# Layer 3 of a graph network: the edges' factors in pieces of 8 tiles, the one-hot ahead of a wait, and gathers 8 quads ahead of PE

## The chip, the cores and the metric

The kernel runs on one core of a Trainium2 chip. The metric is the time of one execution in device microseconds, taken as the median of several runs. The core's engines are TensorE (PE, matmuls; PEld is its weight load), VectorE (DVE), ScalarE (ACT), GpSimd (POOL) and SyncE (SP). Each engine works through its own instructions in order; between engines they wait for one another with semaphores.

## The reference, cut to what matters

Four layers pass messages along 262144 edges between 8192 nodes of 32 features; each ends in a residual sum and a layer norm. The edges are sorted by their target. The change concerns the fourth (layer 3):

```python
def _L3_gnn_ref(node_attr, edge_index, edge_sh, edge_feat, W1, b1, W2, b2, si_w0, si_w1):
    h = jax.nn.relu(edge_feat @ W1 + b1)
    w = (h @ W2 + b2).reshape(e, 4, MUL, MUL)                  # MUL = 8
    w_000, w_011, w_101, w_110 = (w[:, 0], w[:, 1], w[:, 2], w[:, 3])
    s = node_attr[:, :MUL]
    v = node_attr[:, MUL:].reshape(n, MUL, 3)
    s_e, v_e = s[src], v[src]
    sh0, sh1 = edge_sh[:, 0], edge_sh[:, 1:4]
    m0 = ALPHA * (jnp.einsum('ei,eio->eo', s_e * sh0[:, None], w_000)
                  + C110 * jnp.einsum('eim,em,eio->eo', v_e, sh1, w_110))
    m1 = ALPHA * (jnp.einsum('ei,em,eio->eom', s_e, sh1, w_011)
                  + jnp.einsum('eim,eio->eom', v_e * sh0[:, None, None], w_101))
    out0 = jax.ops.segment_sum(m0, dst, num_segments=n) + SI_SCALE * (s @ si_w0)
    out1 = ...
x = _layernorm(x + _L3_gnn_ref(x, edge_index, edge_attr_4, edge_attr_32, ...), axis=-1)
```

So each edge gathers the row of its source (s, 8 numbers, and v, 8 x 3), has 256 weights of its own from a small network over its 32 features, and sends 32 numbers to its target. The products of the row with the edge's four numbers `sh` (s x sh0, the sum of v x sh1, v x sh0) don't need the weights: these are the "factors".

## The kernel before

The edges lie in tiles of 128 (one edge on each partition). Layer 3 has 2048 tiles, in 512 quads of 4 tiles (`q`), in 64 batches of 32 tiles or 8 quads (`s`).

**GpSimd (POOL)** fetches the source rows with one indirect DMA for each tile (L383, in `indirect`), four for each quad. `fetch_rows(q)` issues those of quad q after a wait for PE's weight matmuls of quad q - AHEAD, with AHEAD = 12: so the gathers of the first 12 quads need no wait for PE. `gathers` also waits, at the first tile of each group of 8, until the buffer of the group is free (`taken`; there are four buffers of 32 tiles) and until the group two before has landed.

**PE** has three kinds of matmuls for layer 3. At even q it computes the hidden layer of quads q + 2 and q + 3 (`hidden`, L883), which ACT turns into the activations (relu, L891). For each q it makes the weights of the quad (L907, 4 matmuls of 256 columns, into one of two `w` banks); they wait for ACT and until VectorE has freed the bank (`w_free`). Then it adds up the messages of quad q - 4 (L916, one-hot matrices times products), after VectorE's mark of quad q - 2 at the latest.

**VectorE (DVE)** does in round q, in this order: at q % 8 == 6 the factors of the next batch (below); the last product of quad q - 2 (L931); the reduce of quad q - 1 (L936); then it waits for PE's weights of quad q, multiplies them with the factors (L944, L947, three times L951), and builds the one-hot matrices of the quad (`one_hot`, L505). The mark behind the one-hot is what frees the `w` bank, lets the aggregation go on, and, at the end of a group, frees the gather buffer. Every second round it also takes two quads' sums out of PSUM (L973, L974, L976).

**The factors** of a batch (`factors`, L825 to L836) are six instructions over all 32 tiles: the scale of `sh`, three products, a reduce and a scale. They wait until all four groups of gathers of the batch have landed. One set is computed in each 8 quads, so 64 in all.

**Windows.** Every 64 quads, in the same round as a set of factors (q % 8 == 6), PE shifts the sums to their targets (`windows`, L495) and VectorE and ACT normalize a stripe of nodes (`normalize`, from L454).

**SP** loads the edges' features and `sh` three batches ahead (`fetch`).

**Before the first quad** a loop of 16 rounds (L852 to L858, the "z loop") goes from PE to ACT to PE to VectorE and adds each node's own part. The first hidden layer (L883) comes after it, while POOL's first gathers are under way.

Of the kernel before, what the change touches and what calls it, by code (L numbers as in the profile page):

```python
# [16 lines left out]
OP = mybir.AluOpType  # L17
# [4 lines left out]
P = 128  # L22
# [6 lines left out]
ALPHA = 0.25  # L29
C110 = 1.0 / np.sqrt(3.0)  # L30
# [7 lines left out]
WT = 32  # L38
# [107 lines left out]
def raw_layers(tc, x, a, w0, w1, b1, w2, si, m, bad):  # L146
    nc = tc.nc
    PE, V, A, G, S = (Flow(tc, e, n) for e, n in ((nc.tensor, "pe"), (nc.vector, "dve"), (nc.scalar, "act"),
                                                  (nc.gpsimd, "pool"), (nc.sync, "sp")))
    bank, arena = m["bank"], m["arena"]  # L150
    x_a, x_b, src, row, rel = (m[k] for k in ("x_a", "x_b", "src", "row", "rel"))
    ident, shift, stack, small = (m[k] for k in ("ident", "shift", "stack", "small"))
    iota_s = m["iota_s"]
    ytab, xtab, hist, amat, cmat = (m[k] for k in ("ytab", "xtab", "hist", "amat", "cmat"))
# [37 lines left out]
    cut = Carve()  # L192
# [8 lines left out]
    xg = cut(4, WT, D)  # L201
    oh = cut(4, GT, P, dt=BF)
# [5 lines left out]
    cut = Carve(8192)  # L208
# [5 lines left out]
    cut = Carve()  # L214
# [211 lines left out]
    def gathers(table, ix, s, t0=0, n=WT):  # L426

        if t0 == 0:
            state["n"] += 1
        k = (state["n"] - 1) % 4  # L430
        for t in range(t0, t0 + n):
            ld = g_ld[k][t // TP]
            if t % TP == 0:
                G.after(taken[k][t // TP])
                if len(under_way) >= LAG:
                    G.after(under_way[-LAG])
            indirect(xg[:, k, t, :], table[:, :], ix[:, s * WT + t:s * WT + t + 1]).then_inc(ld.sem, 16)
            ld.n += 16
            if t % TP == TP - 1:
                under_way.append(ld.mark())  # L440
        return k, under_way[-(WT // TP):]
# [62 lines left out]
    def one_hot(o, t, n):  # L504
        return V.e.tensor_tensor(o, iota[:, None, :].to_broadcast([P, n, P]),  # L505
                                 rel[:, t:t + n, None].to_broadcast([P, n, P]), op=OP.is_equal)
# [254 lines left out]
    ef = cut(3, 2, 512)  # L761
    sh = cut(3, WT, 4)
    a0 = cut(2, WT, 16)
    vs = cut(WT, 8, 3)
    a1 = cut(WT, 8)
    vm = cut(2, WT, 3, 8)
    MW = 344
    NP, NO = 6, 6
# [36 lines left out]
                                         a["ea4"][:, 4 * s * WT:4 * (s + 1) * WT]))  # L805
        batch[s] = dict(e=e_in, s=s_in)

    AHEAD = 12
    rows = {}

    def fetch_rows(q):

        if q < NQ:
            G.after(quad.get(q - AHEAD, {}).get("w"))
            rows[q // 8] = gathers(xtab, src, q // 8, q % 8 * 4, 4)

    def factors(s):

        k, landed = rows[s]
        b = batch[s]  # L820
        b["xg"] = k
        shv = sh[:, s % 3]
        u = s % 2
        V.after(b["s"])
        sm = V.mark(V.e.tensor_scalar(shv, shv, ALPHA, None, op0=OP.mult))  # L825
        V.after(*landed, sm)
        xv = xg[:, k]
        v = xv[:, :, 8:].rearrange("p t (i m) -> p t i m", m=3)
        vmk = V.mark(V.e.tensor_tensor(vs, v, shv[:, :, None, 1:4].to_broadcast([P, WT, 8, 3]), op=OP.mult))
        V.e.tensor_tensor(a0[:, u, :, 0:8], xv[:, :, 0:8], shv[:, :, 0:1].to_broadcast([P, WT, 8]), op=OP.mult)  # L830
        V.e.tensor_tensor(vm[:, u].rearrange("p t m i -> p t i m"), v,
                          shv[:, :, None, 0:1].to_broadcast([P, WT, 8, 3]), op=OP.mult)
        V.after(vmk)
        rm = V.mark(V.e.tensor_reduce(a1, vs, AX.X, OP.add))
        V.after(rm)
        b["f"] = V.mark(V.e.tensor_scalar(a0[:, u, :, 8:16], a1, float(C110), None, op0=OP.mult))  # L836


    V.after(c_in)
# [59 lines left out]
    for q in range(NQ + LAG3 + 2):  # L899
# [18 lines left out]
            quad[c]["a"] = PE.mark(ins)  # L918

        prev = (V.sem, V.n)  # L920
        if q % 8 == 6 and q // 8 + 1 < NS:
            s = q // 8 + 1
            factors(s)
        V.after(prev)
        if q < NQ:
            V.after(batch[q // 8]["f"])
        V.after(quad.get(q - NP, {}).get("a"))
        ins = None
        if 0 <= q - 2 < NQ:
# [8 lines left out]
        if q < NQ:  # L938
            k, wp = quad[q]["k"]
            s, u = q // 8, (q // 8) % 2  # L940
            qs = slice((q % 8) * 4, (q % 8) * 4 + 4)
            pq = p[:, q % NP]
            V.after(quad[q]["w"])
            V.e.tensor_tensor(pr[:, q % 2].rearrange("p t (o i) -> p t o i", i=8),  # L944
                              wp[:, :, 128:192].rearrange("p t (o i) -> p t o i", i=8),
                              xg[:, batch[s]["xg"], qs, None, 0:8].to_broadcast([P, 4, 8, 8]), op=OP.mult)
            V.e.tensor_tensor(pq[:, :, 0:128].rearrange("p t (o k) -> p t o k", k=16),  # L947
                              wp[:, :, 0:128].rearrange("p t (o k) -> p t o k", k=16),
                              a0[:, u, qs, None, :].to_broadcast([P, 4, 8, 16]), op=OP.mult)
            for mm in range(3):  # L950
                V.e.tensor_tensor(pq[:, :, 128 + 64 * mm:192 + 64 * mm].rearrange("p t (o i) -> p t o i", i=8),  # L951
                                  wp[:, :, 192:256].rearrange("p t (o i) -> p t o i", i=8),
                                  vm[:, u, qs, mm, None, :].to_broadcast([P, 4, 8, 8]), op=OP.mult)
            ins = one_hot(oh[:, q % NO], 4 * q, 4)
        if ins is not None:
            d = V.mark(ins)
            if q < NQ + 2:
# [498 lines left out]
```

## Time and profile before

| | us |
|---|---|
| median of 3 runs | 7668.28 (7660.74 to 7670.0) |
| the profiled execution | 7583.78 |
| its span in the profile | 7581.8 |
| DVE busy in the span | 4352.7 (57%) |
| PE busy in the span | 5254.6 (69%) |
| POOL busy in the span | 3996.6 (53%) |

The profile is that of one execution, which was some 1.1% faster than the median. Layer 3's first gather starts at 4522.57, and the layer ends with the span.

A line of the timeline has the start in us, the time it took, the engine, the line of the kernel, the operation, what it writes and reads, how many it stands for, and in brackets the idle time before it and who ended that. A line of the groups has busy time and the mean in ns after the first bar, and the idle time before the group's instructions after the second. "issue" is time in which the profile shows no wait; "remote" is a releaser that the profile can't place.

### The profile page before, as it was taken

Reading aid. Unit: us, or ns where it says so; the run is one execution under the profiler, and the core shown is the slowest. Engines: PE = TensorE matmul, PEld = TensorE weight load, DVE = VectorE, ACT = ScalarE, POOL = GpSimd, SP = SyncE. Lnnn points to the kernel's source line nnn. Section 1 sums busy time; section 2 is a strip of 40 time slices with the busy share of each in tenths; the row PEclk is TensorE's granted clock in tenths of the full one; section 3 lists DMA queues with packets and bytes.
Section 4 is the critical chain, followed back from the end, with each engine's and each line's share of the span. In section 5 each row is a group of like instructions: output and inputs, shape, how many; then the busy total and the mean of one; then the engine's idle time right before and its main releaser. Section 6 shows DMA issues by size and latency. Waiting matters only on the chain.

```text
span 7581.8 us, 85791 instructions
## 1 busy us (share of the span) xinstructions
PE 5254.6 (69%) x34036; PEld 3717.5 (49%) x34036; DVE 4352.7 (57%) x8312; ACT 1629.6 (21%) x2812; POOL 3996.6 (53%) x4174
## 2 busy tenths in 40 slices
PE   5326665556555665654544867889989988888998
PEld 2115555555555555553222434555555555555555
DVE  3336676677676767764000005666666667666676
ACT  3213333333333333332000001111111111111111
POOL 3466565656566666650000016666666666666663
PEclk7557677777777777777777877999998999899989
DMA  8416655556555555668999971111111111111111
GB/s 285 149 36 145 144 150 139 145 144 152 145 145 145 144 151 138 152 142 279 428 431 428 386 289 18 28 23 25 24 24 24 24 24 24 24 24 24 25 24 20
DMA packets 290731, 999.29 MB, mean 132 GB/s; under 512 B 99021, under 2 KB 175886, under 8 KB 250638
## 3 DMA queue, kind: packets, MB, share of 16 engines
q1 hardware_dynamic: 155742, 916.89, 32.2%
q0 software_dynamic: 134144, 73.67, 12.2%
q8 instruction: 269, 4.41, 0.2%
q10 hardware_dynamic: 432, 3.15, 0.1%
q14 instruction: 144, 1.18, 0.1%
HBM read 521.39 MB, written 471.99 MB: 131 GB/s over the span
## 4 chain that ended last, share of the span: by engine, by line
PE 55%; another core or an unknown queue 11%; DMA 11%; issue 9%; DVE 8%; ACT 5%; POOL 0%; SPq 0%; DVEq 0%; ACTq 0%; POOLq 0%
PE bank L571 18%; PE bank L916 14%; PE bank L907 11%; DMA f_arena<-famat 7%; PE bank L657 3%; PE bank L883 3%; DMA f_arena<-fcmat 3%; ACT f_arena L576 3%; PE bank L730 2%; PE bank L733 2%; ACT f_arena L575 2%; DVE f_arena L951 1%; DVE f_arena L505 1%; PE bank L495 1%
## 5 line engine op out<-in xcount | busy, mean ns | idle before, releaser
L383 POOL DMA_INDIRECT f_arena<-fxtab,f_src x2048 | 1967.3, 961 | 2099.2 <-DVE f_arena L787 1089.0
L383 POOL DMA_INDIRECT f_arena<-fytab,f_row x2048 | 1962.0, 958 | 1280.5 <-issue 548.2
L571 PE MATMUL bank<-f_arena 64*128 64x128 f32 x16384 | 1566.7, 365 | 963.4 <-ACT f_arena L576 682.8
L571 PEld LDWEIGHTS bank<-f_arena 64*128 64x128 f32 x16384 | 1463.3, 272 | 1100.6 <-issue 938.7
L916 PE MATMUL bank<-f_arena 128*128 128x344 f32 x4096 | 1420.3, 489 | 65.4 <-issue 63.7
L907 PE MATMUL bank<-f_arena 65*128 65x256 f32 x4096 | 1075.3, 405 | 176.2 <-issue 161.0
L916 PEld LDWEIGHTS bank<-f_arena 128*128 128x128 f32 x4096 | 842.8, 207 | 509.3 <-issue 217.5
L907 PEld LDWEIGHTS bank<-f_arena 65*128 65x128 f32 x4096 | 785.2, 198 | 559.3 <-issue 361.0
L575 ACT ACTIVATE f_arena<-bank 128x512 bf16<-128x512 f32 x1024 | 613.0, 599 | 1925.4 <-PE bank L571 816.8
L891 ACT ACTIVATE f_arena<-bank,f_arena 64x512 f32<-64x512 f32 x512 | 351.3, 686 | 2500.1 <-remote 1001.6
L557 DVE TENSOR_TENSOR f_arena<-bank,f_arena 128x1024 f32<-128x1024 f32 x256 | 313.3, 1224 | 759.8 <-PE bank L657 440.4
L505 DVE TENSOR_TENSOR f_arena<-bank,f_rel 128x512 f32<-128x512 f32 (+1 forms) x768 | 660.9, 861 | 139.9 <-ACT f_arena L537 127.7
L944 DVE TENSOR_TENSOR f_arena<-bank,f_arena 128x256 f32<-128x256 f32 x512 | 214.7, 419 | 845.0 <-PE bank L907 324.4
L576 ACT ACTIVATE f_arena<-bank 128x512 f32<-128x512 f32 x1024 | 611.7, 597 | 0.0
L559 DVE TENSOR_TENSOR f_arena<-bank,f_arena 128x2048 f32<-128x2048 f32 x256 | 586.6, 2291 | 8.8
L951 DVE TENSOR_TENSOR f_arena<-bank,f_arena 128x256 f32<-128x256 f32 x1536 | 552.0, 416 | 0.0
L730 PE MATMUL bank<-f_arena,f_x_b 128*32 128x256 f32 x4096 | 293.2, 457 | 344.9 <-DMA f_arena<-famat 344.9
L657 PE MATMUL bank<-f_arena 128*128 128x96 bf16 x2048 | 216.7, 222 | 357.7 <-issue 215.5
L730 PEld LDWEIGHTS bank<-f_arena,f_x_b 128*32 128x32 f32 x4096 | 145.1, 131 | 481.8 <-DMA f_arena<-famat 318.0
L454 DVE TENSOR_TENSOR f_lnf<-bank,f_x_b 128x256 f32<-128x256 f32 x8 | 3.4, 425 | 615.0 <-PE bank L710 615.0
L947 DVE TENSOR_TENSOR f_arena<-bank,f_arena 128x512 f32<-128x512 f32 x512 | 348.8, 681 | 0.0
L657 PEld LDWEIGHTS bank<-f_arena 128*128 128x128 bf16 x2048 | 122.0, 104 | 404.5 <-issue 260.2
(133 smaller groups left out, 3532.6 us busy)
## 6 DMA issues: line engine op xcount, KB each, us to landing
famat<-f_arena SPq DMA_DIRECT2D x256, 1024.0 KB
fcmat<-f_arena SPq DMA_DIRECT2D x256, 512.0 KB
fytab<-f_arena SPq DMA_DIRECT2D x64, 1024.0 KB
f_arena<-fytab,f_row POOLq DMA_INDIRECT x2048
f_arena<-fxtab,f_src POOLq DMA_INDIRECT x2048
f_arena<-laid_ea SPq DMA_DIRECT2D x64, 512.0 KB
f_arena<-laid_ea SPq DMA_DIRECT2D x64, 64.0 KB
f_arena<-laid_xT ACTq DMA_DIRECT2D x1, 1024.0 KB, 8.9
```

The lines of the kernel that those rows point to most:

```text
L383: return G.e.indirect_dma_start(out=dest, out_offset=None, in_=table, in_offset=bass.IndirectOffsetOnAxis(ap=ix, axis=0))
L505: return V.e.tensor_tensor(o, iota[:, None, :].to_broadcast([P, n, P]), rel[:, t:t + n, None].to_broadcast([P, n, P]), op=OP.is_equal)
L559: V.e.tensor_tensor(oh_l[:, b], iota[:, None, :].to_broadcast([P, 16, P]), meta_l[:, pp, k0:k0 + 16, None].to_broadcast([P, 16, P]), op=OP ...
L571: ins = PE.e.matmul(bank[:, bk + h, :].rearrange("p (c s j) -> p c s j", s=64, j=4)[:, :, :, j], oh_l[hs_, b, 4 * q + j, :], oh_k[hs_, b, ...
L575: A.e.activation(st_c[:, b, q], bank[:, bk:bk + 2, 0:256], AF.Copy)
L576: bank_free[units[0] % 2] = am = A.mark(A.e.activation(st_a[:, b, q], bank[:, bk:bk + 2, 256:512], AF.Copy))
L657: ins = PE.e.matmul(bank[:, bk, 3 * c * D:3 * (c + 1) * D], oh[:, h, t, :], xp[:, g % 4, t].rearrange("p c f -> p (c f)"), start=(t == 0), ...
L730: ins = PE.e.matmul(bank[q * D:(q + 1) * D, b, 0:256].rearrange("p (u h j) -> p u h j", h=2, j=4), x_b[:, s, :], mv[:, s], start=(s < 4), ...
L891: quad[q + h] = dict(h=A.mark(A.e.activation(hs[0:64, (q + h) % 4], bank[64 * h:64 * h + 64, 2, :], AF.Relu, bias=b1_s[64 * h:64 * h + 64])))
L907: ins = PE.e.matmul(wp[:, t, :], hs[0:65, q % 4, t * P:(t + 1) * P], w2_s[0:65], start=True, stop=True)
L916: ins = PE.e.matmul(bank[:, g % 2, 0:MW], oh[:, c % NO, t, :], p[:, c % NP, t, :], start=(c % 2 == 0 and t == 0), stop=(c % 2 == 1 and t = ...
L951: V.e.tensor_tensor(pq[:, :, 128 + 64 * mm:192 + 64 * mm].rearrange("p t (o i) -> p t o i", i=8), wp[:, :, 192:256].rearrange("p t (o i) - ...
```

## The change

The gathers run 8 quads ahead of PE instead of 12. The factors are computed for 8 tiles (2 quads) at a time: at every even q VectorE does those of quads q + 2 and q + 3, and waits only until the one group of 8 gathers that these need has landed. The scale of `sh` stays one instruction for each batch. Two helper buffers (`vs`, `a1`) shrink to 8 tiles, so a piece also waits for the end of the piece before it. The one-hot of quad q moves ahead of the wait for PE's weights, so that VectorE's mark of the quad now stands on the third L951. PE's instructions and their order stay, as do ACT's and SP's.

```diff
@@ -761,8 +761,8 @@
-    vs = cut(WT, 8, 3)
-    a1 = cut(WT, 8)
+    vs = cut(8, 8, 3)
+    a1 = cut(8, 8)
...
@@ -805,35 +805,39 @@
-    AHEAD = 12
+    AHEAD = 8
     rows = {}
+    factor = {}
 
     def fetch_rows(q):
 
         if q < NQ:
             G.after(quad.get(q - AHEAD, {}).get("w"))
-            rows[q // 8] = gathers(xtab, src, q // 8, q % 8 * 4, 4)
-
-    def factors(s):
-
-        k, landed = rows[s]
+            rows[q // 2] = gathers(xtab, src, q // 8, q % 8 * 4, 4)
+
+    def factors(r):
+
+        k, landed = rows[r]
+        s, ts = r // 4, slice(r % 4 * 8, r % 4 * 8 + 8)
         b = batch[s]
         b["xg"] = k
-        shv = sh[:, s % 3]
         u = s % 2
-        V.after(b["s"])
-        sm = V.mark(V.e.tensor_scalar(shv, shv, ALPHA, None, op0=OP.mult))
-        V.after(*landed, sm)
-        xv = xg[:, k]
+        if r % 4 == 0:
+            shb = sh[:, s % 3]
+            V.after(b["s"])
+            V.after(V.mark(V.e.tensor_scalar(shb, shb, ALPHA, None, op0=OP.mult)))
+        shv = sh[:, s % 3, ts]
+        V.after(landed[-1], factor.get(r - 1))
+        xv = xg[:, k, ts]
         v = xv[:, :, 8:].rearrange("p t (i m) -> p t i m", m=3)
-        vmk = V.mark(V.e.tensor_tensor(vs, v, shv[:, :, None, 1:4].to_broadcast([P, WT, 8, 3]), op=OP.mult))
-        V.e.tensor_tensor(a0[:, u, :, 0:8], xv[:, :, 0:8], shv[:, :, 0:1].to_broadcast([P, WT, 8]), op=OP.mult)
-        V.e.tensor_tensor(vm[:, u].rearrange("p t m i -> p t i m"), v,
-                          shv[:, :, None, 0:1].to_broadcast([P, WT, 8, 3]), op=OP.mult)
+        vmk = V.mark(V.e.tensor_tensor(vs, v, shv[:, :, None, 1:4].to_broadcast([P, 8, 8, 3]), op=OP.mult))
+        V.e.tensor_tensor(a0[:, u, ts, 0:8], xv[:, :, 0:8], shv[:, :, 0:1].to_broadcast([P, 8, 8]), op=OP.mult)
+        V.e.tensor_tensor(vm[:, u, ts].rearrange("p t m i -> p t i m"), v,
+                          shv[:, :, None, 0:1].to_broadcast([P, 8, 8, 3]), op=OP.mult)
         V.after(vmk)
         rm = V.mark(V.e.tensor_reduce(a1, vs, AX.X, OP.add))
         V.after(rm)
-        b["f"] = V.mark(V.e.tensor_scalar(a0[:, u, :, 8:16], a1, float(C110), None, op0=OP.mult))
+        factor[r] = V.mark(V.e.tensor_scalar(a0[:, u, ts, 8:16], a1, float(C110), None, op0=OP.mult))
...
         prev = (V.sem, V.n)
-        if q % 8 == 6 and q // 8 + 1 < NS:
-            s = q // 8 + 1
-            factors(s)
+        if q % 2 == 0 and q + 2 < NQ:
+            factors(q // 2 + 1)
         V.after(prev)
         if q < NQ:
-            V.after(batch[q // 8]["f"])
+            V.after(factor[q // 2])
...
             pq = p[:, q % NP]
+            one_hot(oh[:, q % NO], 4 * q, 4)
             V.after(quad[q]["w"])
...
-                V.e.tensor_tensor(pq[:, :, 128 + 64 * mm:192 + 64 * mm].rearrange("p t (o i) -> p t o i", i=8),
-                                  wp[:, :, 192:256].rearrange("p t (o i) -> p t o i", i=8),
+                ins = V.e.tensor_tensor(pq[:, :, 128 + 64 * mm:192 + 64 * mm].rearrange("p t (o i) -> p t o i", i=8),
+                                        wp[:, :, 192:256].rearrange("p t (o i) -> p t o i", i=8),
                                   vm[:, u, qs, mm, None, :].to_broadcast([P, 4, 8, 8]), op=OP.mult)
-            ins = one_hot(oh[:, q % NO], 4 * q, 4)
```

## The prediction

> **What bounds the kernel now.** I read the table of slices first, to find layer 3 in the span.
>
> ```profile
> PE   5326665556555665654544867889989988888998
> ...
> DVE  3336676677676767764000005666666667666676
> ...
> POOL 3466565656566666650000016666666666666663
> PEclk7557677777777777777777877999998999899989
> ```
>
> A slice is 189.5 us. VectorE pauses through slices 19 to 23, and from slice 24 on POOL gathers, VectorE works at about 6 tenths and PE at 8 to 9: these 16 slices are layer 3. No engine is full. The table of windows for the steady part (columns: PE, PEld, DVE, ACT, POOL busy, PE clock, DMA share, GB/s) gives sizes:
>
> ```profile
> 4600.00:7500.00 2900.00, 2604.19 (x9081) 1661.94 (x9079) 1990.18 (x5159) 346.75 (x512) 1920.97 (x2000) 0.92 0.13 24
> ```
>
> POOL issues 2000 gathers, 500 quads, so a quad takes 2900 / 500 = 5.80 us (5.75 without the windows of step 3). PE needs less: after the last gather, at 7511 to 7535, quads follow every 4.66 us. The groups of the same stretch:
>
> ```profile
> L383 POOL DMA_INDIRECT f_arena<-fxtab,f_src x2000 | 1921.9, 961 | 995.8 <-issue 550.1 <-PE bank L907 192.6 <-remote 177.4
> ...
> L916 PE MATMUL bank<-f_arena 128*128 128x344 f32 x3977 | 1381.2, 489 | 64.7 <-issue 62.9
> ...
> L907 PE MATMUL bank<-f_arena 65*128 65x256 f32 x4006 | 1051.5, 405 | 176.1 <-issue 161.0 <-DVE f_arena L505 14.2
> ...
> L944 DVE TENSOR_TENSOR f_arena<-bank,f_arena 128x256 f32<-128x256 f32 x499 | 209.2, 419 | 829.0 <-PE bank L907 316.2 <-remote 312.7 <-PE bank L916 136.1
> ```
>
> A gather is 0.96 us plus 0.30 of issue in a row (1.2525 start to start), so four take 5.01 us, and 995.8 us of POOL's idle less 1998 x 0.29 leave about 400 us (0.2 us a gather) in pauses for PE's w (L907). L944, the first product of VectorE, waits 829 us, mostly for PE. Everybody waits for PE, and PE for "issue", which hides what it waits for. The timeline around one burst of factors shows it:
>
> ```profile
> 5597.59 1.07 PE L883 MATMUL bank<-f_arena 32*64 32x512 f32 x4
> ...
> 5601.04 0.43 DVE L944 TENSOR_TENSOR f_arena<-bank,f_arena 128x256 f32<-128x256 f32 x1 [4.92 <-PE bank L907]
> ...
> 5601.28 0.94 POOL L383 DMA_INDIRECT f_arena<-fxtab,f_src  x1 [1.15 <-PE bank L907]
> ...
> 5603.57 0.22 DVE L825 TENSOR_SCALAR f_arena<-f_arena 128x128 f32<-128x128 f32 x1
> ...
> 5608.14 1.40 ACT L891 ACTIVATE f_arena<-bank,f_arena 64x512 f32<-64x512 f32 x2 [17.33 <-remote]
> ...
> 5608.23 0.43 DVE L944 TENSOR_TENSOR f_arena<-bank,f_arena 128x256 f32<-128x256 f32 x1
> ...
> 5608.47 0.94 POOL L383 DMA_INDIRECT f_arena<-fxtab,f_src  x1 [2.44 <-remote]
> ```
>
> The matmul of L883 ends at 5598.66, but ACT, which waits for nothing else but w's before it, gets going at 5608.14, together with POOL, 9.5 us later. So PE's releases arrive late while gathers stream, and several together soon after POOL pauses. POOL runs on its credit of 12 quads, pauses, is released, and so on: 12 gathers every 17.25 us or 16 every 23.0 where I followed it, both 1.436 us a gather and 5.75 us a quad. I take the gather stream with its late releases to be the bound. That makes the burst, 4.07 us from 5603.57 to the next instruction at 5607.64, free here: 5608.23 is when the w's come anyway.
>
> At the 7 windows (every 64 quads) it is not free:
>
> ```profile
> 5368.95 0.22 DVE L825 TENSOR_SCALAR f_arena<-f_arena 128x128 f32<-128x128 f32 x1
> ...
> 5376.98 4.87 PE L495 MATMUL bank<-f_arena,f_shift 128*128 128x256 f32 x14 [4.79 <-DVE f_arena L505]
> ...
> 5383.85 0.94 POOL L383 DMA_INDIRECT f_arena<-fxtab,f_src  x1 [6.14 <-PE bank L907]
> ```
>
> The burst of that round starts at 5368.95, L944 follows at 5373.55, and only after VectorE's rest come the matmuls of the window (L495), for which PE stood 4.79 us. POOL pauses 6.14 us there against some 2 to 3 otherwise. Sixty-four quads take about 372 us against 64 x 5.75 = 368, an excess of 4.2 us by finer marks.
>
> The start:
>
> ```profile
> 4522.57 0.95 POOL L383 DMA_INDIRECT f_arena<-fxtab,f_src  x1 [1089.02 <-DVE f_arena L787]
> ...
> 4575.21 0.29 DVE L858 TENSOR_TENSOR f_arena<-bank,f_x_b 128x128 f32<-128x128 f32 x1 [8.11 <-remote]
> ...
> 4581.35 0.94 POOL L383 DMA_INDIRECT f_arena<-fxtab,f_src  x1 [0.30 <-issue]
> ...
> 4589.60 1.97 PE L883 MATMUL bank<-f_arena 32*64 32x512 f32 x4 [2.07 <-DVE f_arena L858]
> ...
> 4599.10 0.95 POOL L383 DMA_INDIRECT f_arena<-fxtab,f_src  x1 [16.80 <-PE bank L907]
> ```
>
> Forty-eight gathers stream from 4522.57 to 4582.3; the rounds of the z loop, 1.4 us at first, wait 8.11 us each meanwhile; PE's first hidden layer is at 4589.60 and POOL's 49th gather, the first that waits for a w, at 4599.10.
>
> [...] the trace has a clock of 0.50 through the start (4522 to 4599), 0.92 in the steady part.
>
> **The change, part by part.** The sum is made against the profiled execution, 7583.78 us (span 7581.8 and 2.0 around it). The median, 7668.28, is 84.5 us or 1.1% higher; savings are carried to it unscaled.
>
> 1. Eight quads ahead at the start. Thirty-two gathers stream instead of 48: 16 x 1.2525 = 20.0 us less, to 4562.6. The z loop has then done 2.3 rounds less (8.4 us each while gathers stream), and runs these afterwards in about 2 us each: 20.0 - 4.5 = 15.5 us sooner, the first hidden layer at about 4574. Bounds: 10 (the loop's remaining rounds stay slow) and 20 (all follows the stream); the 23 us of 16 x 1.436 are just beyond. Taken: -15.5.
>
> 2. Eight quads ahead at the end. The last 12 quads ran without gathers at 4.65 us; now the last 8. Four quads x (5.75 - 4.65) = +4.4 us.
>
> 3. Pieces and one-hot at the windows. The burst of 4.07 us in the window's round becomes one piece. [...] Instructions overlap a little (burst: 4.32 busy in 4.07), so 1.35 to 1.4 elapsed. That is 2.7 us sooner. The one-hot of 0.68 us, now run while VectorE waits for w, adds some 0.2 there. L495 comes 2.9 us sooner, 7 x 2.9 = 20 us; it can't exceed the excess, 7 x 4.2 = 29, and can be 0 if POOL's stream, not the burst, sets the pause. Taken: -19.
>
> 4. Pieces elsewhere. VectorE's work grows: 256 x 1.59 + 64 x 0.22 = 421 us against 64 x 4.33 = 277, so +144 us over 512 quads, 0.28 a quad. VectorE's 4.1 us of work a quad becomes 4.4 against 5.75. What hides it is the wait at L944, 829 us in 499 quads. If the cover is gone everywhere, pieces cost 256 x 1.4 - 64 x 4.07 = +98 us; if the bursts were exposed where I saw none, losing them gains as much as 57 x 2.7 = 154. Taken: 0. The late thing is then still PE's release.
>
> 5. The one-hot ahead of the wait. It takes 0.6 us from between w and VectorE's mark, which frees w's bank and the aggregation. Bounds: 0, and 512 x 0.6 = 307 us if that mark were last in every quad. After a bunched release I find VectorE's second mark at up to 6.55 us and PE ready for it at about 6.9, so it isn't last. Taken: 0.
>
> 6. Waits of the pieces. A piece at an even quad q needs the gathers of q+2 and q+3. VectorE is in order, so L931, L936, the one-hot and the products of quad q queue behind, and PE's next w behind these. When PE has released w of q-3, POOL may issue up to q+5, so by rate the data of q+3 were issued two quads or more (10 us) before. I take 0; a hold would come under rival D. POOL's and SP's queues keep their order, SP's loads still come three batches ahead, and the row and wait of the scale stay one per batch.
>
> Sum: -15.5 + 4.4 - 19 = -30.1, so 7583.78 becomes 7553.7, and the median 7638.
>
> **Rivals.** A, the forecast, 7638, from 7615 (start -18, windows -29, and a few of the pieces' gains) to 7655 (start -10 + 4.4, windows -7). Chance 0.54.
>
> B, larger gain: step 5 wrong. The mark is last once in each cycle of credit, some 125 cycles of 23 us, since 6.55 and 6.9 us differ by little and bunches vary. Then 125 x 0.6 = 75 us come on top of some of A's: about 7562. For it speaks L944's <-PE bank L916 and the nearness of the two figures; against it that two patterns of cycle give the same 5.75. Chance 0.18.
>
> C, no change: the window's pause is POOL's running dry plus its own 4.87 us of matmuls, and not the burst, and the start gains 10 only, less 4.4 at the end: 7663, at most 15 us from before. For it: gathers are 2048 x 1.436 = 2941 us of the 3059 whatever VectorE does, and less lead is in hand. Against it: PE stands 4.79 us for VectorE ahead of L495. Chance 0.14.
>
> D, slower: after a bunched release VectorE works three quads back to back to catch up. Before, one round in eight had a burst; now every second has a piece of 1.4 us, which delays the second mark from 6.55 to 6.55 + 1.4 - 0.65 = 7.3 us, past PE's 6.9. From the point where this mark passes PE's readiness each cycle grows. If half of 125 cycles lose the whole 0.75 us it is +47; with the credit now 8 quads a cycle has fewer quads and there are more of them (180: +68). With the -11 of steps 1 and 2: 7704 to 7725. For it: VectorE then fills 4.4 of 5.75 us and no other engine's work grows. Against it: 829 us of waiting in L944. Chance 0.14.
>
> That the change doesn't do what it says I leave out: in the instruction order of the changed kernel the pieces stand every second quad and the one-hot ahead of L944's wait.
>
> **How the numbers follow.** The likeliest is A, 7638, on its own 7615 to 7655. B ends at 7562, so a low end of 7560 takes in most of it, and 7672 takes in C; left out are D and B's far end, 0.2 in all. Within 0.2% is 15 us either way (about what a measurement can tell from no change). Faster: A and B, 0.72. Same: C, 0.14. Slower: D, 0.14.
>
> **What would show it.** Step 1: the first gather to wait is the 33rd, with L883 first near 4574 (counted from a first gather at 4522.6). Step 3: the idle of PE before L495 falls by about 2.9 us in each window, and POOL's pause there with it. Step 4: DVE busy near 4497 us against 4352.7, L944's wait down by some 144. Steps 4 and 5: 5.75 us a quad between windows. A pace of 5.6 would show B, of 5.85 or more D, with PE waiting for VectorE's marks ahead of L907. The forecast is wrong if the pace of a quad depends on how many gathers are ahead of PE, which nothing in this trace varies.

## The result and the profile after

| | kernel before | changed kernel |
|---|---|---|
| median of 6 runs, us | 7660.09 (7657.75 to 7670.0) | 7638.15 (7630.33 to 7658.1) |
| ratio of the runs | | 0.9971, 95% interval 0.9957 to 0.9985 |
| the profiled execution, us | 7583.78 | 7658.1 |
| first gather of layer 3, in the span | 4522.57 | 4580.49 |
| from there to the end of the span | 3059.2 | 3075.7 |

The changed kernel is 22 us faster by its runs, and the median is the forecast's 7638. The forecast had counted 30 us from a median of 7668 for the kernel before, which six runs put at 7660; so 8 of these 30 us are missing.

The two profiled executions say the opposite: the changed kernel's took 74 us more. Of these, 58 lie ahead of layer 3, in code that is the same in both; the other 16.5 lie in layer 3. The profiled execution before was 76 us below its median, that of the changed kernel the slowest of its six. Layer 0 also gathers in a stream of 2048, and the change doesn't touch it. Its first and last gather in the kernel before, and then in the changed one:

```profile
271.44 0.95 POOL L383 DMA_INDIRECT f_arena<-fytab,f_row  x1 [80.43 <-DMA fytab<-f_arena]
...
3432.61 0.94 POOL L383 DMA_INDIRECT f_arena<-fytab,f_row  x1 [0.30 <-issue]
```

```profile
274.38 0.94 POOL L383 DMA_INDIRECT f_arena<-fytab,f_row  x1 [81.28 <-DMA fytab<-f_arena]
...
3498.61 0.94 POOL L383 DMA_INDIRECT f_arena<-fytab,f_row  x1 [0.30 <-issue]
```

The stream took 3161.2 us in one execution and 3224.2 in the other: the same code was 2.0% slower. One profile from each kernel can't settle a difference of 22 us here, nor one of pace below some 2%; it can show which waits moved inside layer 3.

The table of slices of the changed kernel:

```profile
PE   5326565656566665655445777998999989898998
...
DVE  3336666666676766665000005676667676677666
...
POOL 3466565656566565651000006666666666666664
...
PEclk6556766677666667677777887999898998998988
```

Layer 3 looks as before: PE at 8 to 9 tenths, no engine full. The steady part in the table of windows (PE, PEld, DVE, ACT, POOL busy, PE clock, DMA share, GB/s) has PE's clock at 0.90 instead of 0.92:

```profile
4640.00:7574.00 2934.00, 2656.34 (x9084) 1709.63 (x9083) 2040.41 (x6102) 347.36 (x514) 1893.23 (x2000) 0.90 0.12 24
```

Its groups (busy time and mean in ns, then the idle time before them and what ended it):

```profile
L383 POOL DMA_INDIRECT f_arena<-fxtab,f_src x2016 | 1908.9, 947 | 1067.6 <-issue 556.1 <-PE bank L911 203.6 <-remote 183.4
...
L920 PE MATMUL bank<-f_arena 128*128 128x344 f32 x4016 | 1397.4, 492 | 18.2 <-issue 17.3
...
L911 PE MATMUL bank<-f_arena 65*128 65x256 f32 x4039 | 1098.5, 419 | 187.4 <-DVE f_arena L955 182.4 <-issue 4.7
...
L948 DVE TENSOR_TENSOR f_arena<-bank,f_arena 128x256 f32<-128x256 f32 x505 | 211.1, 418 | 823.6 <-remote 294.2 <-PE bank L911 272.5 <-PE bank L920 243.7
...
L495 PE MATMUL bank<-f_arena,f_shift 128*128 128x256 f32 (+1 forms) x98 | 38.7, 577 | 50.5 <-DVE f_arena L979 36.2 <-issue 7.3 <-DVE f_arena L977 7.0
```

The reader is to see two things. First, L948, VectorE's first product, still waits 824 us for PE: the cover of the pieces is there. Second, PE's w matmuls (L911) now wait 182 us for L955, the mark of VectorE, where before they waited 161 us for "issue"; but in all they stood 187 us, against 176 before, so it is mostly the name of the wait that changed. One piece of the steady part, from its first product to the next instruction of VectorE:

```profile
5598.40 0.35 DVE L833 TENSOR_TENSOR f_arena<-f_arena 128x192 f32<-128x192 f32 x1
...
5599.60 0.25 DVE L934 TENSOR_TENSOR f_arena<-f_arena 128x96 f32<-128x96 f32 x1
```

For the windows the view of groups of the kernel before has

```profile
L495 PE MATMUL bank<-f_arena,f_shift 128*128 128x256 f32 (+1 forms) x98 | 34.1, 522 | 52.8 <-DVE f_arena L976 29.4 <-DVE f_arena L505 23.4
```

so PE stood 52.8 us ahead of the windows' matmuls before, and 50.5 us after.

The timeline of the start:

```profile
4580.49 0.94 POOL L383 DMA_INDIRECT f_arena<-fxtab,f_src  x1 [1080.94 <-DVE f_arena L787]
...
4614.52 0.29 DVE L862 TENSOR_TENSOR f_arena<-bank,f_x_b 128x128 f32<-128x128 f32 x1 [7.44 <-remote]
...
4619.17 0.95 POOL L383 DMA_INDIRECT f_arena<-fxtab,f_src  x1 [0.31 <-issue]
...
4630.07 1.97 PE L887 MATMUL bank<-f_arena 32*64 32x512 f32 x4 [0.43 <-DVE f_arena L862]
...
4639.56 0.94 POOL L383 DMA_INDIRECT f_arena<-fxtab,f_src  x1 [19.45 <-PE bank L911]
```

From the first gather to PE's first hidden layer (L887) it is 49.6 us now; before, 67.0. POOL's 33rd gather waits 19.45 us, as its 49th waited 16.80.

The timeline of one window of the changed kernel:

```profile
5414.02 1.07 PE L887 MATMUL bank<-f_arena 32*64 32x512 f32 x4
...
5415.99 0.22 DVE L828 TENSOR_SCALAR f_arena<-f_arena 128x128 f32<-128x128 f32 x1
...
5423.43 1.39 ACT L895 ACTIVATE f_arena<-bank,f_arena 64x512 f32<-64x512 f32 x2 [15.87 <-remote]
...
5423.52 0.42 DVE L948 TENSOR_TENSOR f_arena<-bank,f_arena 128x256 f32<-128x256 f32 x1 [4.81 <-remote]
...
5426.36 5.23 PE L495 MATMUL bank<-f_arena,f_shift 128*128 128x256 f32 x14 [7.03 <-DVE f_arena L979]
...
5433.60 0.94 POOL L383 DMA_INDIRECT f_arena<-fxtab,f_src  x1 [5.16 <-PE bank L911]
```

The piece starts at 5415.99 and is over at 5417.58. VectorE then stands 4.81 us for PE's w. The hidden layer's matmul of L887 ended at 5415.09, and ACT starts at 5423.43, 8.3 us later: the late release comes at the end of the round, not the piece. L495 follows at 5426.36 after PE stood 7.03 us. All seven windows of the changed kernel are like this: VectorE waits 4.0 to 5.4 us for a w in the window's round or in the one before it, and PE stands 6.0 to 8.7 us. In the kernel before, VectorE went on from the burst without a wait in four of the seven, this window among them.

Layer 3 of the two profiles, cut at POOL's marks, with its first wait for PE at 4599.10 (49th gather) before and 4639.56 (33rd) after, and the last gather at 7499.07 and 7595.69:

| part, us | before | after | difference |
|---|---|---|---|
| first gather to POOL's resuming | 76.5 | 59.1 | -17.5 |
| from there to the last gather | 2900.0, for 2000 gathers | 2956.1, for 2016 | +56.2 |
| last gather to the end | 82.7 | 60.5 | -22.2 |

Sixteen gathers more in the middle part are 16 x 1.45 = 23.2 us of the 56.2; the other 33 are pace, 1.466 us a gather against 1.450. That is 1.1% slower, where the same code of layer 0 was 2.0% slower in this execution.

### The profile page after: what moved, and what is told of

It reads as the page before. It is cut to its first block, busy times and chain, and to the rows that moved or that the text cites. A ratio compares the mean times of both kernels' runs of the same rounds, so it can differ in the third digit from the quotient of the medians.

```text
span 7656.2 us, 86689 instructions
## 1 busy us (share of the span) xinstructions
PE 5377.4 (70%) x34036; PEld 3808.2 (50%) x34036; DVE 4401.0 (57%) x9272; ACT 1628.4 (21%) x2812; POOL 3962.6 (52%) x4174
## 3 DMA queue, kind: packets, MB, share of 16 engines
q1 hardware_dynamic: 155742, 916.89, 30.8%
## 4 chain that ended last, share of the span: by engine, by line
PE 47%; another core or an unknown queue 15%; DVE 14%; DMA 11%; issue 7%; ACT 6%; POOL 0%; SPq 0%; DVEq 0%; ACTq 0%; POOLq 0%
PE bank L571 16%; PE bank L920 12%; PE bank L911 10%; DMA f_arena<-famat 7%; DVE f_arena L955 3%; ACT f_arena L576 3%; DMA f_arena<-fcmat 3%; ACT f_arena L575 2%; PE bank L887 2%; PE bank L730 2%; DVE f_arena L951 2%; PE bank L733 2%; DVE f_arena L505 2%; DVE f_arena L948 1%
## 5 line engine op out<-in xcount | busy, mean ns | idle before, releaser
L383 POOL DMA_INDIRECT f_arena<-fxtab,f_src x2048 | 1939.1, 947 | 2158.0 <-DVE f_arena L787 1080.9
L571 PE MATMUL bank<-f_arena 64*128 64x128 f32 x16384 | 1596.9, 369 | 980.3 <-issue 552.0
L571 PEld LDWEIGHTS bank<-f_arena 64*128 64x128 f32 x16384 | 1480.8, 275 | 1095.8 <-issue 910.4
L911 PE MATMUL bank<-f_arena 65*128 65x256 f32 x4096 | 1114.1, 419 | 187.4 <-DVE f_arena L955 182.4
L911 PEld LDWEIGHTS bank<-f_arena 65*128 65x128 f32 x4096 | 811.8, 205 | 581.2 <-DVE f_arena L955 283.9
L948 DVE TENSOR_TENSOR f_arena<-bank,f_arena 128x256 f32<-128x256 f32 x512 | 214.1, 418 | 831.7 <-remote 294.2
L955 DVE TENSOR_TENSOR f_arena<-bank,f_arena 128x256 f32<-128x256 f32 x1536 | 550.7, 414 | 0.0
L657 PE MATMUL bank<-f_arena 128*128 128x96 bf16 x2048 | 250.2, 252 | 330.0 <-issue 187.3
L657 PEld LDWEIGHTS bank<-f_arena 128*128 128x128 bf16 x2048 | 143.8, 117 | 422.4 <-issue 289.3
L951 DVE TENSOR_TENSOR f_arena<-bank,f_arena 128x512 f32<-128x512 f32 x512 | 348.5, 681 | 0.0
```

Of the source, the lines that this page charges most:

```text
L383: return G.e.indirect_dma_start(out=dest, out_offset=None, in_=table, in_offset=bass.IndirectOffsetOnAxis(ap=ix, axis=0))
L571: ins = PE.e.matmul(bank[:, bk + h, :].rearrange("p (c s j) -> p c s j", s=64, j=4)[:, :, :, j], oh_l[hs_, b, 4 * q + j, :], oh_k[hs_, b, ...
L657: ins = PE.e.matmul(bank[:, bk, 3 * c * D:3 * (c + 1) * D], oh[:, h, t, :], xp[:, g % 4, t].rearrange("p c f -> p (c f)"), start=(t == 0), ...
L911: ins = PE.e.matmul(wp[:, t, :], hs[0:65, q % 4, t * P:(t + 1) * P], w2_s[0:65], start=True, stop=True)
L955: ins = V.e.tensor_tensor(pq[:, :, 128 + 64 * mm:192 + 64 * mm].rearrange("p t (o i) -> p t o i", i=8), wp[:, :, 192:256].rearrange("p t ( ...
```

## The experiments

In all later runs the kernel before took 6470 to 6500 us instead of 7660. They fell on four chips; which chip the first runs had isn't known. That it was another one is likely, but a state of a chip that had passed by then isn't excluded. "Chip" in this comparison stands for either. Because of the noise ahead of layer 3, most kernels leave layers 0 to 2 out and let layer 3 work on the input rows. In the table "stream" is from the first gather to the last, "drain" from the last gather to the end of the span, both from the profile's timeline; "pauses" is POOL's idle time between gathers beyond the usual 0.30 us.

The four chips differ a little: the whole kernel before took 6497 us (median) on that of b3, a3, a3_ahead12 and a3_ohlate, 6483 on that of a3_16 and a3_nogath, 6476 to 6479 on that of a3_4 and w_4, and 6477 on that of the other whole kernels.

| kernel | us, median (range) | stream | drain | quads left at the last gather | pauses |
|---|---|---|---|---|---|
| b3: before, layer 3 alone | 2857.38 (2856.51 to 2862.46) | 2587.3 | 79.6 | 10 | 11.5 |
| a3: changed, layer 3 alone | 2816.45 (2815.86 to 2818.62) | 2575.1 | 46.1 | 4 | 0 |
| a3_ahead12 | 2816.14 (2810.85 to 2817.84) | 2570.8 | 46.0 | 4 | 0 |
| a3_ohlate | 2814.84 (2813.23 to 2817.2) | 2573.4 | 46.3 | 4 | 0 |
| a3_16: pieces of 16 tiles | 2831.25 (2830.65 to 2834.04) | 2580.5 | 56.7 | 6 | 1.1 |
| a3_4: pieces of 4 tiles | 2794.35 (2792.31 to 2795.61) | 2562.7 | 38.7 | 2 | 0 |
| w_before: whole, before | 6477.38 (one run) | 2585.6 | 76.1 | 10 | 12.9 |
| w_after: whole, changed | 6433.04 (6429.64 to 6437.39) | 2570.8 | 45.3 | 4 | 0 |
| w_ahead12: whole | 6433.86 (6430.8 to 6438.3) | 2575.1 | 45.4 | 4 | 0 |
| w_b_ohearly: whole | 6474.65 (6468.04 to 6477.93) | 2581.5 | 77.7 | 10 | 10.9 |
| w_4: whole, pieces of 4 tiles | 6419.52 (6416.05 to 6420.9) | 2565.7 | 38.3 | 2 | 0 |

**The base and the changed kernel, layer 3 alone.** The edit: the loops of layers 0 to 2 go, and the rows are stored as they come.

```diff
-    for g in range(GG + 2):
...
-    for n, (l, c) in enumerate(seq):
...
+    xm = V.mark(V.e.tensor_copy(x_b, x_a))
+    S.after(xm)
+    x_st.add(S.e.dma_start(xtab.rearrange("(d p) f -> p d f", p=P), x_b))
```

> The kernel before with layers 0 to 2 left out: layer 3 works on the input rows as they are, so that its time can be read without the 4520 us ahead of it. Theory 1 (the prediction: the start and the windows gain, the pace of a quad stays): first gather to end 3059 us in the profile, as in the whole kernel (3059.2); the time is that plus a few hundred us of preparation. Theory 2 (the profile of the changed kernel taken at its word: start -17.5 us, but a slower pace, layer 3 3075.7 us against 3059.2): the same for this kernel. Both need this as the base of the next three.

> The changed kernel with layers 0 to 2 left out in the same way. Theory 1: 30 us less than the kernel before in the same form (range 20 to 45). Theory 2: 16 us more, and what the whole kernel gained was in the layers that the change doesn't touch. A third theory, that the profiler's own records slow the changed kernel, which has 960 more instructions on VectorE: faster in the timed runs, slower in the profile.

The changed kernel took 41 us less, inside theory 1's range of 20 to 45. But it was not theory 1's reason: in the kernel before layer 3 took 2667 us from first gather to end where 3059 were expected, and POOL, apart from the windows, didn't pause once. So neither theory's picture of pauses held on this chip.

**The whole kernels there.** No edit.

> The whole kernel before, unchanged, beside its time of 6497 us on the chip of the layer-3-alone runs and 7660 us where the prediction was made. If late releases by PE (gathers pausing after 12 or 16) are a matter of the kernel's earlier layers, its profile shows pauses in layer 3 again (some 370 us of them, 5.75 us a quad) whatever the total. If they belong to a chip, a chip with the short total shows 5.0 us a quad, set by POOL's issue alone, and pauses only at the windows (8 of them, 11 us), and layer 3 takes 2667 us from first gather to end.

> The whole changed kernel, unchanged. On a chip with pauses: ratio 0.997 again (-22 us), as first measured. On a chip without pauses: the gain of layer 3 alone, 41 us in 2857, comes to 6497 - 41 = 6456, ratio 0.9937; made up of about 12 us of windows' pauses and the rest at the end, where the last gather is 8 quads instead of 12 from the end of PE's work.

The ratio was 0.9932 (0.9918 to 0.9945), where 0.9937 was written down for a chip without pauses. The timeline of the kernel before, around its first window:

```profile
4216.32 0.96 DVE L829 TENSOR_TENSOR f_arena<-f_arena 128x768 f32<-128x768 f32 x1 [3.99 <-DMA f_arena<-fxtab,f_src]
...
4223.98 5.92 PE L495 MATMUL bank<-f_arena,f_shift 128*128 128x256 f32 x14 [6.87 <-DVE f_arena L976]
...
4231.90 0.94 POOL L383 DMA_INDIRECT f_arena<-fxtab,f_src  x1 [2.21 <-PE bank L907]
...
4233.88 1.07 PE L883 MATMUL bank<-f_arena 32*64 32x512 f32 x4
...
4235.01 1.40 ACT L891 ACTIVATE f_arena<-bank,f_arena 64x512 f32<-64x512 f32 x2 [2.28 <-PE bank L883]
```

ACT starts L891 0.06 us after the matmul of L883 ended (4234.95). In the first profile that took 9.5 us, with the same program. It is so throughout: here ACT follows within 0.12 us after each of layer 3's 256 hidden layers; in the first profile 125 of them took over 1 us, and one took 10.9.

That matmuls which ran late are recorded as early is not the reason. The trace also has the times at which PE's marks (its semaphore) went up. In layer 3 of the first profile, after the start, 369 of the 1055 on record come within 0.15 us of the one ahead, although the matmuls that they stand on end at least 1.00 us apart: so marks of work done before were held back and came in a bunch. Here it is 0 of 1245. In the first profile layer 0's stream of gathers has 212 of these, and the stretch between the two streams, without gathers, none. Late releases are thus no property of the kernel, and gathers alone don't make them: POOL issues them here faster than there. What does make them was not found.

Without late releases POOL issues a gather each 1.25 us, 5.0 us a quad, with no stop but at the windows, and VectorE waits for gathers too, not only for PE. The groups of the kernel before, and then of the changed one, over the whole of layer 3:

```profile
L383 POOL DMA_INDIRECT f_arena<-fxtab,f_src x2048 | 1948.9, 952 | 1645.5 <-DVE f_arena L787 1007.9 <-issue 543.1 <-DMA f_arena<-fxtab,f_src 50.3
...
L944 DVE TENSOR_TENSOR f_arena<-bank,f_arena 128x256 f32<-128x256 f32 x512 | 215.6, 421 | 249.4 <-PE bank L907 230.9
...
L829 DVE TENSOR_TENSOR f_arena<-f_arena 128x768 f32<-128x768 f32 x64 | 61.8, 965 | 231.0 <-DMA f_arena<-fxtab,f_src 229.2
```

```profile
L383 POOL DMA_INDIRECT f_arena<-fxtab,f_src x2048 | 1947.9, 951 | 1633.6 <-DVE f_arena L787 1009.8 <-issue 521.7 <-DMA f_arena<-fxtab,f_src 53.0
...
L948 DVE TENSOR_TENSOR f_arena<-bank,f_arena 128x256 f32<-128x256 f32 x512 | 213.8, 418 | 54.8 <-PE bank L911 48.2
...
L833 DVE TENSOR_TENSOR f_arena<-f_arena 128x192 f32<-128x192 f32 x256 | 93.0, 363 | 348.1 <-DMA f_arena<-fxtab,f_src 346.3
```

Before, VectorE waits 231 us at the burst's first product for gathers and 249 us at L944 for PE. After, 348 us for gathers and 55 us for PE: it follows the gathers closely. That is what the smaller piece changes. A burst in round q needs the gathers up to quad q + 9, so the last burst is in round 502 and waits for the last gather of all:

```profile
6399.34 0.94 POOL L383 DMA_INDIRECT f_arena<-fxtab,f_src  x1 [0.30 <-issue]
...
6401.81 0.96 DVE L829 TENSOR_TENSOR f_arena<-f_arena 128x768 f32<-128x768 f32 x1 [5.01 <-DMA f_arena<-fxtab,f_src]
```

Round 502 and nine more then remain. In the changed kernel the last piece is in round 508:

```profile
6386.47 0.95 POOL L383 DMA_INDIRECT f_arena<-fxtab,f_src  x1 [0.30 <-issue]
...
6388.84 0.36 DVE L833 TENSOR_TENSOR f_arena<-f_arena 128x192 f32<-128x192 f32 x1 [1.95 <-DMA f_arena<-fxtab,f_src]
```

Six quads fewer at 4.65 us (the pace without gathers in the first profile) are an estimated 27.9 us, of a drain that fell by 30.8. The rest of the 44 is the windows: POOL's pauses of 12.9 us, one of them ahead of the gather at 4231.90 above, are gone.

**The other two parts of the change.** Lead back to 12; one-hot and mark back behind the products; and the one-hot alone moved in the kernel before.

```diff
-    AHEAD = 8
+    AHEAD = 12
```

```diff
-            one_hot(oh[:, q % NO], 4 * q, 4)
             V.after(quad[q]["w"])
...
-                ins = V.e.tensor_tensor(pq[:, :, 128 + 64 * mm:192 + 64 * mm].rearrange("p t (o i) -> p t o i", i=8),
+                V.e.tensor_tensor(pq[:, :, 128 + 64 * mm:192 + 64 * mm].rearrange("p t (o i) -> p t o i", i=8),
...
+            ins = one_hot(oh[:, q % NO], 4 * q, 4)
```

> The changed kernel, layer 3 alone, with gathers 12 quads ahead again and pieces and early one-hot kept. Theory 1: the start's gain goes, +11 us against the changed kernel in this form, pace unchanged at 17.45 us per 12 gathers. Theory 2 (a pause of POOL costs about the same after 12 gathers as after 16, so a shorter credit costs pace): the pauses come after 16 gathers again every 23.0 us, layer 3 gets 30 us faster in the pace and 13 us slower at the start, so 15 to 20 us less than the changed kernel in this form.

> The changed kernel, layer 3 alone, with the one-hot behind the products again, so that the mark stands behind it. Theory 1 (the mark isn't last in the steady part): +1 us for each of seven windows, +7 at most. Rival (the mark is last once in each cycle of POOL's credit, about 165 cycles): 165 x 0.6 = +100 us. Rival (last in no cycle, and the one-hot fills the wait for nothing): 0.

> The whole changed kernel with gathers 12 quads ahead again. On a chip where PE's releases come late while gathers stream (kernel before near 7660 us): by the prediction only the start's -11 goes, ratio to before 0.9985; by the rival that the shorter credit costs pace (12 gathers per pause instead of 16), the profile shows pauses after 16 gathers again, layer 3 some 20 us shorter than in the changed kernel, ratio 0.9945. On a chip without late releases (kernel before near 6480): POOL never waits for PE, so the lead is of no account, ratio 0.9932 as the changed kernel's, layer 3 2616 us.

> The whole kernel before with only the one-hot moved ahead of the wait for PE's weights. On a chip with late releases: by the prediction VectorE's mark is not last, so some 0.5 us for each of 7 windows, ratio 0.9995 to 1; by its rival B (mark last once in each cycle of credit) -75 us, ratio 0.990. On a chip without: POOL sets the pace and VectorE's mark matters only at the windows and after the last gather: -7 x 0.5 and 12 quads x up to 0.6, in all -4 to -11 us, ratio 0.9983 to 0.9994; if instead PE's 69 us of waiting for L505 were on the path, -60 us, ratio 0.991.

Against the changed kernel in the same form they gave -0.3 us (lead) and -1.6 us (one-hot); the whole kernel with lead 12 has ratio 0.9933 (0.9919 to 0.9946) to the kernel before, the same as with lead 8; the one-hot alone moved in the kernel before 0.9996 (0.9988 to 1.0004). The 4 to 11 us that the one-hot alone was expected to give didn't come: 2.4 us, with an interval that takes in zero. On a chip without late releases each of the two parts is worth nothing by itself, which leaves the gain to the pieces; the two weren't undone together. On a chip with late releases nothing was tried, since no run fell on one: which part makes the 22 us there, and whether a lead of 8 costs pace there, stays open.

**Piece size.** Sixteen tiles, and four tiles with gathers tracked in groups of four.

```diff
...
-        if q % 2 == 0 and q + 2 < NQ:
-            factors(q // 2 + 1)
+        if q % 4 == 2 and q + 2 < NQ:
+            factors(q // 4 + 1)
...
```

```diff
-    TP = 8
+    TP = 4
...
-    LAG = 2
+    LAG = 4
...
-        if q % 2 == 0 and q + 2 < NQ:
-            factors(q // 2 + 1)
+        if q + 1 < NQ:
+            factors(q + 1)
...
```

> The changed kernel, layer 3 alone, with pieces of 16 tiles (4 quads) instead of 8, at q % 4 == 2. If the gain without late releases comes from how many quads are still to do when the last gathers land (9 with 32 tiles, 3 with 8, 5 with 16) and from the windows: about 2 quads x 4.65 = 9 us more after the last gather than with 8 tiles, 46 to 55 us, windows' pauses 0 to 3 us, so 2825 us (2857 with 32, 2816 with 8). If the number of VectorE instructions mattered, 16 tiles would be faster than 8.

> The changed kernel, layer 3 alone, with pieces of 4 tiles (one quad), computed in round q for quad q + 1, and gathers tracked in groups of 4 tiles. By the drain explanation (time after the last gather is set by how many quads still need work when it lands: 9 with 32 tiles, 5 with 16, 3 with 8): 1 to 2 quads less, so 46 us after the last gather become 37 to 41, and 2816 becomes 2807 to 2811. Against it stands VectorE, whose work grows by about 0.25 us a quad to 4.65 of 5.0: if windows' pauses of POOL come back (7 of 1 to 2 us), 2815 to 2830. On a chip with late releases: slower than the kernel before in this form if VectorE's share counts.

The drain follows the quads that are left (the expectations count one less for 32, 16 and 8 tiles, without the round of the piece itself): 79.6, 56.7, 46.1 and 38.7 us for 10, 6, 4 and 2. With four tiles its size was met (37 to 41 expected), with sixteen it was just missed (46 to 55 expected, 56.7 found; 2825 us expected in all, 2831.25 found). VectorE's extra work cost nothing that shows. The end of the stream with four tiles:

```profile
2754.59 0.94 POOL L383 DMA_INDIRECT f_arena<-fxtab,f_src  x1 [0.30 <-issue]
...
2756.87 0.26 DVE L652 TENSOR_TENSOR f_arena<-f_arena 128x96 f32<-128x96 f32 x1 [1.00 <-DMA f_arena<-fxtab,f_src]
```

The last piece waits 1.00 us only, and two quads remain. But with four tiles the time fell by 22 us, not by 5 to 9: the stream itself was 12.4 us shorter, with gathers of 947 ns on average against 953. That part was not expected, and it was measured on another chip than a3, on which the whole kernel before was 0.33% faster: an estimated 8 us of a stream of 2575.

As a whole kernel:

> The whole kernel with pieces of 4 tiles in round q for quad q + 1 (the form that took 2794 us as layer 3 alone against 2857 before and 2816 with 8 tiles). On a chip without late releases: 6477 - 63 = 6414 us, ratio to the kernel before 0.990 (the changed kernel: 0.993); if the gain is tied to the chip or the short form, 0.993 again. On a chip with late releases: VectorE has some 0.5 us a quad more to do than before, hidden by its wait for PE, and the end has two quads less to drain, ratio 0.994 to 0.997; above 1 if VectorE's work is on the path there.

It took 6419.52 us (6416.05 to 6420.9), ratio 0.9909 (0.9893 to 0.9926), the fastest of all versions; the changed kernel had 0.9932 on its chip. These two intervals overlap, and both comparisons of the sizes, this one and a3_4 with a3, go across chips. The traces help: in w_4 and w_after the stream of layer 0, the same code in both, took 2579.7 and 2580.1 us, so these two executions compare well. From w_after to w_4 layer 3's stream fell by 5.1 us and the drain by 7.0. So the drain repeats, and some 5 of the 12.4 us of stream; why the stream should shorten at all stays open.

**Without gathers.** All gathers but those of the first 32 quads left out; later quads use the rows of these again.

```diff
-        if q < NQ:
+        if q < 32:
             G.after(quad.get(q - AHEAD, {}).get("w"))
             rows[q // 2] = gathers(xtab, src, q // 8, q % 8 * 4, 4)
+        elif q < NQ:
+            rows[q // 2] = rows[q // 2 - 16]
```

> The changed kernel, layer 3 alone, with the gathers of all but the first 32 quads left out (the rows that lie in the four buffers are used again). If POOL's issue of gathers (5.0 us a quad) sets the pace on a chip without late releases, a quad takes PE's 4.65 us or VectorE's 4.5: 480 x 0.35 = 168 us less, about 2650 us. If PE or VectorE set it together with the gathers, the pace stays near 5.0 and the time within 30 us of 2816. On a chip with late releases: 480 x (5.8 - 4.65) = 550 us less than the changed kernel in this form there, and no late release.

It took 2664.12 us (2662.61 to 2664.44), 152 less than a3, which ran on another chip (168 expected). The table of windows over a stretch of 446 quads:

```profile
400.00:2500.00 2100.00, 2096.08 (x8125) 1392.42 (x8124) 1839.98 (x5457) 311.77 (x461) 0.00 (x0) 1.00 0.05 16
```

PE is busy 2096 of 2100 us at a granted clock of 1.00: 4.71 us a quad is PE's own pace, and POOL's 5.0 was the bound above it.

## Why the prediction was right, and where it wasn't

The direction was right, and the time lies in the range. That it lies on the forecast itself is luck: -30.1 us were forecast and -21.9 measured between the medians, and the median before came out 8.2 us lower with six runs than with three, which makes up the difference. Of the steps, this is what stands behind them:

- Step 1, the start. Forecast -15.5 us with bounds of 10 and 20; the profile has -17.5. The mechanism is there as described: rounds of the z loop wait 7.4 us while gathers stream and 0.9 to 1.1 us soon after. On chips without late releases it is nothing, as the runs with a lead of 12 show (-0.3 us in a3_ahead12 against a3, +0.8 in w_ahead12 against w_after).
- Step 2, the end. Forecast +4.4; the table of parts has 23.2 us more stream and 22.2 less drain, +1.0.
- Step 3, the windows: -19 forecast. This step failed on the profile. PE's standing ahead of L495 fell by 2.3 us in all, not by 20, and POOL's seven pauses there from 39.8 to 36.3 us. In four of the seven windows before VectorE did go straight on from the burst, but with a piece in its place it waits for a late w in all seven windows instead. That is close to rival C, by which the pause came from elsewhere than the burst. On the other chips pauses did go, 12.9 us of them, since there the burst came last with nothing behind it: in all seven windows of w_before it first waits 3.9 to 5.7 us for the gathers, and VectorE then goes on without a wait.
- Step 4, the pieces elsewhere. A piece took 1.2 us elapsed in the steady part (5598.40 to 5599.60 above), not 1.35 to 1.4. DVE's busy time rose by 48 us (4352.7 to 4401.0), not 144: I added single durations, which did rise by 147 us, but busy time counts overlapping instructions once. L948 waits for PE as much as before, so the pieces are hidden. The pace in the profile is not 5.75: POOL pauses after 12 gathers about every 17.45 us, 5.82 a quad, and 33 us are lost in all. That lies between the forecast and the 5.85 named as rival D's sign, and three explanations stand. Rival D itself is one; it is weakened by PE's w matmuls, which stood only 11 us longer than before in all. The shorter credit is another (one run of 16 gathers where there were 62); but before, a run of 12 took 17.25 us and one of 16 took 23.02, both 1.44 a gather, so the length of a run by itself cost nothing there. The third is the execution, in which layer 0's unchanged stream was 2.0% slower too; that alone would be enough. No run on that chip tells them apart.
- Step 5, the one-hot. Forecast 0; measured -0.04% (-0.12 to +0.04) alone, and none when undone, where PE's releases aren't late. Rival B was about late ones, so these runs don't test it; its sign, a pace of 5.6, isn't in the profile.

Two figures of the working were off, neither by enough to matter. A gather took 1.4375 us in both patterns (17.25 / 12 and 23.0 / 16), not 1.436. And B and D counted 125 cycles of credit, where the trace has 163 pauses, after 12 gathers, 16 or 4. The 1.59 us that a piece keeps VectorE busy was my estimate, and it came out well. A straight line through the products of 256 and 768 elements in the kernel before (L830 420 ns, L829 960 ns) gives an estimated 353 and 218 ns for those of 192 and 64; the changed kernel's profile has 351 (L833) and 219 (L834). The strided product (L835) took 486 ns, where a quarter of the burst's 1496 is 374. With the reduce (L838, 329) and the scale (L840, 200) the five add up to 1.585 us.

So on the chip of the forecast the sum -15.5 + 4.4 - 19 had one term shown, one small, and one that the profile doesn't show, and the profile's layer 3 is 16.5 us longer where 22 us were gained. The number was met by a sum that isn't proved. What the prediction left out altogether is the reach of a burst: that it ties VectorE to the gathers of nine quads ahead, so that ten quads are left when the last gather lands. It would have given most of the 31 us of drain that the other chips show. The prediction saw the drain only as quads without gathers. Its step 6 asked whether the gathers have landed when the pieces need them, and not the same of the bursts.

## What to carry to other kernels

When a consumer works in batches on streamed data, count how many units are still to do when the last transfer lands; that drain shrank with each smaller batch here (79.6, 56.7, 46.1 and 38.7 us), and the extra instructions cost nothing that shows, since the consumer still waited for the stream (348 us in w_after). Undo each part of a change by itself before crediting it: here the two parts that looked active in the trace were worth nothing (-0.3 and -1.6 us when undone), on the chips where they were tried. Before crediting a small difference between two profiles to a change, compare a stretch of code that the change doesn't touch. And a mechanism read from one trace may belong to the chip: run the unchanged kernel elsewhere before building on it.

## What the runs showed of the hardware that was not expected

- The same kernel took 7660 us in the first runs and 6470 to 6500 on the four chips of all later ones. In the profiles of before and w_before, 1106 us apart, layer 0's stream of gathers took 3161 against 2580 us and layer 3, from its first gather on, 3059 against 2662: 979 of the 1106 lie in the two stretches with gathers. The stretch between them, without gathers, took 1089 against 1008, so something is slower there too, and that isn't explained.
- On the first, ACT began up to 10.9 us after the hidden layer's matmuls were over while gathers streamed, and PE's marks came in bunches; on another, 0.12 us at most, and no bunch.
- A gather's issue, 1.25 us, is nearly the same on both (mean duration 961 and 952 ns, 18 us over 2048), so POOL's own pace explains next to nothing of the difference.
- PE's mean clock with late releases was 0.92 in the steady part of the kernel before and 0.90 in that of the changed one. Without them it was 0.95 (w_before) and 0.96 (w_after) over the stream of gathers, and 1.00 with no gathers at all (a3_nogath, 400 to 2500). Whether the clock is a cause of the difference or follows from PE's standing was not tested.
